# The second image's 3x3 convolution in transformed tiles of two rows by four columns

## The chip, the cores and the metric

One core of a Trainium2 chip runs the whole program. The metric is device microseconds from start to end of one execution; the time before is the median of three runs. Profiles come from one execution each, and their times are counted from the start of its span.

Engine names are those of the profile: PE is TensorE's products and PEld its weight loads, DVE is VectorE, ACT is ScalarE, POOL is GpSimd, SP is the queue that issues most transfers.

## What is computed

Two images of 256 channels and 64x64 pixels pass through two residual layers. Each layer normalises its input over groups of channels first.

```python
# layer 0: x += attention with 8 heads over all 4096 pixels
x = x + attention0(group_norm(x))
# layer 1, on h = group_norm(x):
q, k, v = c1x1(h, conv1), c1x1(h, conv2), c1x1(h, conv3)
ctx   = sa(blockify(q * hd**-0.5 + pos), blockify(k + pos), blockify(v))   # "first attention", groups of 64 pixels
feats = relu(c1x1(ctx, lr_W) * scale + shift)
qx, kx = two 1x1 layers each, with scale, shift and relu, of feats          # fq1, fq2 and fk1, fk2
vx    = c1x1(feats, sr_fv)
feats2 = relu(c1x1(sa(qx, kx, vx), sr_W) * scale + shift)                   # "second attention"
f_conv = per-head mixture of q, k, v by fc_w
out_conv = conv3x3(f_conv, dep_w, grouped)                                  # linear in h
x = x + rate1 * unblock(feats2) + rate2 * out_conv
```

Since q, k and v are linear in h, the mixture and the grouped 3x3 are one dense 3x3 convolution of h with 256 channels in and out; the kernel builds its weights itself.

## The kernel before

**Stages.** The images follow each other. For each: statistics and `project0` (the products `p_wk`, `p_wq`, `pv` of layer 0), `attention0` (its score products `ring`, its value products `av`, the exponent on ACT), then `layer1_first` (first attention, tiles named `lr`) and `layer1_second` (second attention, tiles named `sr`, together with the 3x3). In layer 1 the 4096 pixels are eight tiles `t` of 512 columns (eight image rows); `xts[t]` holds the residual `x` of tile `t`.

**A tile of the second attention.** `branch` makes `phq`, then `hq` on ACT, `prq`, then `rq`; the same for k. `group_attention` makes values (`pvs`), scores (`sp`), the softmax on DVE and ACT (`nm`, `e`, `den`, reciprocal, `e`), turns it on PE (`at`), copies it into a block-diagonal `bd` on DVE, and makes `pc`, which ACT turns into `res`.

**The 3x3.** Normalised pixels lie in `xp`, a zero-bordered image that `to_image` fills from the tiles. `conv_transform` and `conv_step` compute outputs in tiles of two rows by two columns from four row positions r and four column positions q. A step `(s, q)` handles a strip s of 16 rows and one q. `conv_transform` makes column combinations `col` (one POOL instruction, L1022) and row combinations `v` (four, L1026). `conv_step` makes 16 products of 256 columns into `mm`, four PSUM banks with a single buffer (L1036), drains them into `z` with one ACT copy and four DVE additions or subtractions (L1043 to L1047), and adds `z` to `xts` with strides of two (L1059, L1063, L1065). There are 16 steps per image.

```python
for r in range(4):
    for m in range(2):
        for k in range(KC):
            nc.tensor.matmul(mm[:, m, r, :], wf[:, k, 4 * r + q, m * P : (m + 1) * P],
                             v[r // 2][:, r % 2, k, :], start=k == 0, stop=k == KC - 1)
```

Weights `wf` (16 positions) are built on DVE in image 0 (`conv_weights`, L957), passed through memory (`wf_kept`), and fetched again for image 1.

**What sets the order.** Each engine works through its own queue in a fixed order. In `layer1_second` the order on PE is that of the program text (`manual_schedule`); a planner orders DVE, ACT, POOL and SP by its own cost estimates and by `issue_after`. `spots` says at which of three places of a tile a step `conv()` stands, and `images` in which tile further parts of `xp` are written. Step n issues the transform of step n+1. `give(n)` adds `rate1 * res + x` and writes the output of tile n once its strip is complete. Buffers come from rotating pools: `w4` (12 buffers of 4 KB per partition, for `v`, `z`, `hq`, `rq`, `res` and others), `xpool` (nine tiles), `cpool` (one, for `col`), `vpool` (one, for `wf`).

**The seams.** Between stages PE has little to hide behind. At the start, statistics (`pm`, `pv`, a square root on ACT) lead to the normalised `xn` and to `p_wk`; `fold_scores` makes the three small products `pt_place`, `pt_meet`, `pt_key` in between. `Stats.spread` makes a deviation `d` from `mean`. Between the two attentions of image 1, `feats` must be whole before `phq`.

Of the kernel before, what the change touches and what calls it, by code (L numbers as in the profile page):

```python
# [41 lines left out]
def direct_layers(ctx: ExitStack, tc: tile.TileContext, a: dict, out: bass.AP, bad: bass.AP):  # L42
# [19 lines left out]

    def open_banks(name, first):
        stack = ExitStack()
        places = range(first, 8)
        psum.update(
            turn=0, first=first,
            banks={i: stack.enter_context(tc.tile_pool(name=f"{name}_{i}", bufs=1, space=PSUM)) for i in places},
        )
        return stack  # L70
# [35 lines left out]
    def load_layer0(b):  # L106
        both = w4([P, 2, KC, NH0 * HD0], f"wqk0_{b}")
        w0 = {"wk0": both[:, 0], "wq0": both[:, 1]}
        for nm in w0:
# [4 lines left out]
            for k in range(KC):  # L114
                by_head = (by_row if b else rows)[:, k, :].rearrange("p (h m) -> p h m", m=2 * HD0)[:, :, 0:HD0]
                dst = w0[nm][:, k, :].rearrange("p (h m) -> p h m", m=HD0)
                if b:
                    nc.gpsimd.dma_start(out=dst, in_=by_head)
                else:
                    nc.scalar.copy(dst, by_head)  # L120
# [22 lines left out]
    nc.gpsimd.memset(eps, 1e-5)  # L143

# [178 lines left out]
    class Stats:  # L323
# [22 lines left out]
        def spread(self, ks):  # L346
            d = self.d[:, ks]
            nc.vector.tensor_sub(d, self.mv[:, ks, 0], self.mean[:, ks])
            nc.vector.tensor_mul(d, d, d)
            nc.vector.tensor_add(d, d, self.mv[:, ks, 1])  # L350
# [4 lines left out]
        def deviations(self, ks, pv):  # L355
            nc.scalar.activation(self.rstd[:, ks], pv, AF.Sqrt, bias=eps)
            nc.vector.reciprocal(self.rstd[:, ks], self.rstd[:, ks])

    def group_stats(xts, tagn):
# [8 lines left out]
        st.means(both, bank([P, KC], f"pm_{tagn}"), nc.vector.tensor_copy)  # L368
        st.spread(both)
# [3 lines left out]
        st.deviations(both, pv)  # L373
# [50 lines left out]
    def project0(b, xn, w0):  # L424

        def heads4(nm, g):
            for t in range(NT):
# [4 lines left out]
                for k in range(KC):  # L432
                    nc.tensor.matmul(  # L433
# [4 lines left out]
                nc.scalar.activation(pair[:, 0, :], pq, AF.Identity, bias=bias)  # L438
# [6 lines left out]
                )  # L445

        heads4("wk0", 0)
# [556 lines left out]
    kept = {}  # L1004
# [24 lines left out]
    def conv_step(b, xts, wf, v, s, q, pacc, behind_products=None):  # L1029
# [17 lines left out]
        nc.vector.tensor_sub(z[:, 1], z[:, 1], mm[:, :, 3, :])  # L1047
        bias = kept["bias"][1]
        for half in range(2):
            xs = xts[2 * s + half].rearrange("p m (i r j c) -> p m i r j c", i=4, r=2, c=2)  # L1050
            for r in range(2):
# [3 lines left out]
                for c in range(2):  # L1055
# [8 lines left out]
                    elif (q, c) in ((2, 1), (3, 1)):  # L1064
                        nc.vector.tensor_sub(dst, dst, zs)  # L1065

# [22 lines left out]
    def group_attention(nm, q, k, tokens, wv, out, busy=False, apart=False, more=None, split=False, fill=None, ends=None):  # L1089
# [36 lines left out]
        for t in range(4):  # L1126
            for c in range(KC):
                for par in range(2):
                    dst, n = place_of(t, par)
                    nc.tensor.matmul(  # L1130
                        dst, q[:, c, n], k[:, c, n], start=c == 0 and (t == 0 or not more),
                        stop=not more and c == KC - 1, skip_group_check=bool(more),
                    )
# [35 lines left out]
        for tt in range(2):  # L1169
            rows = slice(64 * tt, 64 * tt + 64)  # L1170
            nc.vector.tensor_copy(
# [48 lines left out]
    def layer1_first(b, put, check, st, groups):  # L1220
# [53 lines left out]
        with tc.manual_schedule(engines={E.PE, E.Activation, E.DVE, E.Pool}):  # L1274
# [7 lines left out]
            st.means(second, bank([P, 1], f"pm_l1_{b}"), nc.vector.tensor_copy)  # L1282
            st.spread(second)
# [17 lines left out]
        with tc.manual_schedule(engines={E.PE}):  # L1301

            before = None
            for t in range(NT + 1):
# [25 lines left out]
                before = parts  # L1330

# [4 lines left out]
    def layer1_second(b, xts, feats, mean, rstd, shift, pacc, following):  # L1336

        xp = apool.tile([P, KC, PADW, PADW], F32, tag="A", name=f"xp_{b}")
        for k in range(KC):
# [3 lines left out]
            nc.gpsimd.memset(xp[:, k, 1 : PADW - 1, 0 : PADW : PADW - 1], 0.0)  # L1343

        def to_image(t, both=False):
            for k in range(KC):
                dst = xp[:, k, 1 + 8 * t : 9 + 8 * t, 1 : 1 + W]
                src = xts[t][:, k, :].rearrange("p (r w) -> p r w", w=W)
                if both and k == 1:
# [7 lines left out]
        turns = [divmod(n, 4) for n in range(4 * NT // 2)]  # L1357
# [6 lines left out]
            t: (0, 1, 2) if t < 2 else (0, 1) for t in range(NT - 1)  # L1364
        }
        images = {1: range(5), 3: (5, 6), 4: (7,)} if b == 0 else {0: (3, 4), 1: (5,), 2: (6,), 3: (7,)}

        def conv(behind_products=None):
# [3 lines left out]
            if done + 1 < len(turns):  # L1372
                ahead[done + 1] = conv_transform(b, xp, *turns[done + 1])
            conv_step(b, xts, wf, ahead.pop(done), *turns[done], pacc, behind_products)
            done += 1

        def give(n):
# [3 lines left out]
            for m in range(KC):  # L1381
                nc.vector.scalar_tensor_tensor(
                    res[:, m, :], res[:, m, :], wts["rate1"], xts[n][:, m, :], ALU.mult, ALU.add
                )
# [5 lines left out]
        if b:  # L1390
            with tc.issue_after(kept["feats"].ins):
                for t in range(3):
                    to_image(t, True)
            ahead[0] = conv_transform(b, xp, *turns[0])
        pending, then = None, following()
        for t in range(NT):
# [5 lines left out]
            def branch(one, two, col1, col2, nm, between=None):  # L1402
                hid = w4([P, KC, T], f"h{nm}_{nt}")
                ph = [bank([P, T], f"ph{nm}_{nt}_{m}") for m in range(KC)]
                for k, m in ((0, 0), (0, 1), (1, 0), (1, 1)) if t == 0 else ((0, 0), (1, 0), (0, 1), (1, 1)):
# [3 lines left out]
                    if k == KC - 1:  # L1409
                        bn_relu(hid[:, m, :], ph[m], col1, m)  # L1410
# [21 lines left out]
            with tc.manual_schedule(engines={E.PE, E.DVE} if near else {E.PE}):  # L1432
                q = branch("fq1", "fq2", V_FQ1, V_FQ2, "q")
# [4 lines left out]
                for tt in images.get(t, ()):  # L1438
                    to_image(tt)
# [6 lines left out]
                if b == 0 and t == 2:  # L1446
                    conv()
                res = w4([P, KC, T], f"res_{nt}")
# [14 lines left out]
                next(parts)  # L1463
# [30 lines left out]
            for n in sorted(n for n in results if done >= 4 * (n // 2 + 1)):  # L1494
# [7 lines left out]
    def following():  # L1502
# [21 lines left out]
        st.means(both, bank([P, KC], "pm_l0_1"), nc.vector.tensor_copy)  # L1524
        st.spread(both)
# [10 lines left out]
    for b in range(B):  # L1536
        xts = x_first if b == 0 else ahead["xts"] + load_x(1, range(NT - 1, NT))
        w0 = w0_first if b == 0 else ahead["w0"]
        with open_banks(f"ps0_{b}", 0):
# [9 lines left out]
            next(fold, None)  # L1549
            held = project0(b, xn, w0)  # L1550
# [574 lines left out]
```

## Time and profile before

| what | value |
|---|---|
| median of three runs | 3026.41 us (3025.38 to 3028.41) |
| the profiled execution | 3024.22 us, span 3022.4 us |
| mean granted clock of PE | 0.998 |
| busy: PE, DVE, ACT, POOL | 98%, 81%, 77%, 28% of the span |
| image 0: attention of layer 0 | about 112 to 1120 us |
| image 0: layer 1 | about 1120 to 1528 us |
| image 1: attention of layer 0 | about 1640 to 2624 us |
| image 1: first attention, second attention with 3x3 | about 2624 to 2729 us, 2729 to 3015 us |
| product step L1036, image 1 | 512 records in 16 steps, mean duration 381 ns, overlapping |
| POOL: one `col`, one `v`, image 1 | 2146 ns, 1319 ns |
| DVE: one drain L1044 to L1047 | 678 to 688 ns |

Busy shares are averages over stages with different limits. Durations of single instructions overlap with their neighbours on the same engine, so the distance between starts is what a row of them costs. A product in fp32 stands in the trace as two records. The rows of one engine's waits name what came last before the wait ended.

### The profile page before, as it was taken

To read this page: it belongs to the slowest core of one execution; us is meant where nothing else is said; L and a number is where in the kernel's file an instruction comes from. 1 tells how busy PE (TensorE), PEld (TensorE's weight loads), DVE (VectorE), ACT (ScalarE), POOL (GpSimd) and SP (SyncE) were. 2 spreads that over 40 slices of the span, in tenths; PEclk is the share of its full clock that TensorE was granted. 3 is DMA by queue.
4 is the path that set the end of the run, shared out by engine and by line. 5 is a ranking of instruction groups with operands and counts; after the bars stand their busy time and mean duration, and the time that the engine had idled before them with its cause. 6 is when DMAs were issued, how large, how long until landed. Compare 5 with 4: busy or idle time off the path is not lost.

```text
span 3022.4 us, 64069 instructions
## 1 busy us (share of the span) xinstructions
PE 2963.0 (98%) x25161; PEld 1850.1 (61%) x25161; DVE 2443.4 (81%) x3111; ACT 2341.5 (77%) x3288; POOL 843.3 (28%) x930
## 2 busy tenths in 40 slices
PE   7999999999999999999999999999999999999998
PEld 4565556665565656577765555666555565576765
DVE  4698998999899999856647989989988899935543
ACT  2699999999999994622237999999999999844333
POOL 1022222322223230065401223222222222306440
PEclk9999999999999999999999999999999999999999
DMA  7979779897897761230169688797888976700000
GB/s 263 278 138 183 148 158 173 158 185 155 169 179 156 157 137 36 76 141 31 49 222 265 131 172 166 158 178 148 172 169 161 185 159 128 175 13 4 22 15 23
DMA packets 246662, 425.55 MB, mean 141 GB/s; under 512 B 99096, under 2 KB 110156, under 8 KB 244172
## 3 DMA queue, kind: packets, MB, share of 16 engines
q0 software_dynamic: 96960, 237.57, 40.8%
q1 hardware_dynamic: 149244, 183.51, 22.0%
q8 instruction: 199, 3.26, 0.5%
q14 instruction: 115, 0.94, 0.1%
q10 hardware_dynamic: 144, 0.26, 0.0%
HBM read 120.08 MB, written 68.39 MB: 62 GB/s over the span
## 4 chain that ended last, share of the span: by engine, by line
PE 87%; DVE 5%; DMA 3%; ACT 2%; issue 1%; SPq 0%; ACTq 0%; DVEq 0%; POOLq 0%
PE ring L567 32%; PE av L582 29%; PE mm L1036 7%; PE p_wk L433 2%; PE pv L456 2%; PE p_wq L433 2%; DVE prep L957 2%; PE prq_sr L1417 2%; PE prk_sr L1417 2%; PE pvs_sr L1106 2%; PE phk_sr L1406 1%; PE phq_sr L1406 1%; PE ring L582 1%; PE pvs_lr L1106 1%; PE py L1243 1%
## 5 line engine op out<-in xcount | busy, mean ns | idle before, releaser
L573 ACT ACTIVATE es<-ring 128x512 f32<-128x512 f32 (+2 forms) x1574 | 1202.3, 909 | 35.4 <-PE ring L567 23.3
L567 PE MATMUL ring<-q,k 128*128 128x512 f32 x4096 | 1083.9, 407 | 7.3 <-ACT es L573 5.4
L619 DVE TENSOR_TENSOR e<-e,es 128x1024 f32<-128x1024 f32 (+1 forms) x942 | 1028.8, 1153 | 28.4 <-ACT es L573 27.4
L567 PEld LDWEIGHTS ring<-q,k 128*128 128x128 f32 x4096 | 731.2, 188 | 382.7 <-ACT es L573 116.4
L573 ACT ACTIVATE v<-ring 128x512 f32<-128x512 f32 (+2 forms) x1036 | 785.6, 896 | 15.6 <-PE ring L567 7.5
L582 PE MATMUL av<-es,v 128*32 128x256 f32 (+1 forms) x9648 | 722.1, 389 | 0.0
L619 DVE TENSOR_TENSOR e<-e,v 128x1024 f32<-128x1024 f32 (+1 forms) x624 | 669.1, 1128 | 18.3 <-ACT v L573 17.6
L582 PE MATMUL av<-v 128*32 128x256 f32 x6224 | 506.0, 389 | 0.0
L582 PEld LDWEIGHTS av<-es,v 128*32 128x32 f32 x9648 | 325.2, 109 | 263.8 <-issue 105.1
L582 PEld LDWEIGHTS av<-v 128*32 128x32 f32 x6224 | 222.2, 109 | 169.8 <-issue 70.3
L1036 PE MATMUL mm<-v,wf 128*128 128x256 f32 x1024 | 227.6, 380 | 2.0 <-DVE z L1047 2.0
L629 POOL DMA_DIRECT2D es<-es x116 | 99.0, 853 | 438.5 <-ACT es L573 412.7
L1036 PEld LDWEIGHTS mm<-v,wf 128*128 128x128 f32 x1024 | 192.9, 190 | 33.7 <-issue 6.9
L1026 POOL TENSOR_TENSOR v<-col 128x512 f32<-128x512 f32 x128 | 165.3, 1317 | 172.8 <-ACT rk_sr L1195 40.3
L629 POOL DMA_DIRECT2D acc<-es x126 | 129.5, 1033 | 116.4 <-ACT es L573 32.1
L1043 ACT COPY z<-mm 128x512 f32<-128x512 f32 x32 | 18.7, 585 | 179.1 <-PE mm L1036 179.1
L627 POOL DMA_DIRECT2D es<-es x20 | 11.4, 568 | 508.6 <-ACT es L573 241.1
L629 POOL DMA_DIRECT2D es<-v x74 | 63.1, 853 | 291.1 <-ACT v L573 265.6
L1044 DVE TENSOR_TENSOR z<-z,mm 128x512 f32<-128x512 f32 x32 | 21.9, 686 | 125.3 <-ACT z L1043 124.9
L629 POOL DMA_DIRECT2D v<-es x114 | 115.3, 1011 | 24.7 <-ACT es L573 8.9
L629 POOL DMA_DIRECT2D acc<-v x86 | 87.5, 1017 | 81.9 <-DMA acc<-es 35.5
L1022 POOL TENSOR_TENSOR col<-xp 128x1152 f32<-128x1152 f32 x32 | 69.3, 2165 | 66.6 <-DVE xp L1487 55.4
(252 smaller groups left out, 2639.2 us busy)
## 6 DMA issues: line engine op xcount, KB each, us to landing
acc<-es POOLq DMA_DIRECT2D x122, 512.0 KB, 6.3
acc<-v POOLq DMA_DIRECT2D x78, 512.0 KB, 6.2
es<-es POOLq DMA_DIRECT2D x136, 256.0 KB, 4.2
v<-es POOLq DMA_DIRECT2D x134, 256.0 KB, 5.3
k<-wk_halves SPq DMA_DIRECT2D x64, 512.0 KB
q<-wq_halves SPq DMA_DIRECT2D x256, 128.0 KB
v<-v POOLq DMA_DIRECT2D x88, 256.0 KB, 4.8
es<-v POOLq DMA_DIRECT2D x86, 256.0 KB, 3.9
```

What stands on the lines that cost most here:

```text
L433: nc.tensor.matmul(pq, w0[nm][:, k, g * P : (g + 1) * P], xn[:, k, n], start=k == 0, stop=k == KC - 1)
L456: nc.tensor.matmul(pv[:, j, :], xn[:, k, n0 : n0 + P], w0["wv0"][:, k, :], start=k == 0, stop=k == KC - 1)
L567: touch(nc.tensor.matmul(sc[:, i, :], held["k", g // 2][:, j * P : (j + 1) * P], held["q", g, u // 2][:, u % 2, :], start=True, stop=True, ...
L573: nc.scalar.activation(dst, sc, AF.Exp, scale=SC0), set(range(at % BANKS, at % BANKS + m))
L582: note(nc.tensor.matmul(dst[HD0 * u : HD0 * u + HD0, n], lhs, rhs(u)[:, n], start=start, stop=stop))
L619: nc.vector.tensor_add(dst[:, s, :], dst[:, s, :], src)
L629: nc.gpsimd.dma_start(out=dst, in_=src, accum_op=ALU.add)
L1022: (nc.gpsimd.tensor_add if plus else nc.gpsimd.tensor_sub)(col, cols(one), cols(two))
L1026: (nc.gpsimd.tensor_add if plus else nc.gpsimd.tensor_sub)(dst, rows(one), rows(two))
L1036: nc.tensor.matmul(mm[:, m, r, :], wf[:, k, 4 * r + q, m * P : (m + 1) * P], v[r // 2][:, r % 2, k, :], start=k == 0, stop=k == KC - 1,)
L1106: nc.tensor.matmul(pv[:, i, :], tokens(c, 2 * half + i), wv[:, c, :], start=c == 0, stop=c == KC - 1)
L1417: nc.tensor.matmul(pr[m], wts[two][:, k, m * P : (m + 1) * P], hid[:, k, :], start=k == 0, stop=k == KC - 1)
```

## The change

For image 1 alone, the 3x3 works on tiles of two rows by four columns: six column positions q instead of four, on strips of 32 rows instead of 16. That is 2 strips x 6 = 12 steps, in the order q = 0 to 5 and then 5 to 0, each again with 16 products of 256 columns.

- **Column phases.** `x` and `xp` of image 1 are laid out by column modulo 4. `layer1_first` copies each tile of `x` into that layout on DVE while the first attention runs (`xphase`), `to_image` writes it (images 0 to 2 half on DVE and half on ACT, 3 and 4 on DVE, all ahead of the second attention; 5 to 7 in tiles 1 and 2), and `give` reads it back into column order. `rate1` is multiplied into `res` by an instruction of its own.
- **Transform.** `col` needs a POOL instruction of 1088 elements, two DVE instructions of 544 and one of 1088; `v` is four POOL instructions as before.
- **Step.** Products go to `mm[:, r, :, m, :]`, four pieces of 64 columns in a bank. Each `z` is added to up to four phases of four tiles: 16 instructions of 256 elements for q = 1 to 4, four for q = 0 and 5.
- **Weights.** Two more column positions are made from the four in image 0 (`wider_weights`, tiles 3 and 4, 16 DVE instructions and eight writes on SP). `WideWeights` keeps four positions and fetches the others when one is used up.
- **Order.** In both images, tile 0 makes `hq` and `hk` first; image writes in later tiles are issued after the first layer's rows. Additions of a step may be held until after the next drain (`held`); image 0's first step stands between scores and softmax. At the start three idle products run on arriving `x` and two more around the statistics, the `wk0` copies stand before the square root, the exponent's table is loaded by a one-column activation `warm`, and `pt_place`, `pt_meet`, `pt_key` move behind `p_wk`. `means_and_spread` makes `d` from PSUM directly. The last tile's scores loop over channels first. Image 1's tile 0 of `x` is loaded later, its buffer being used as `stage`.

```diff
+        idle = bank([P, T], "idle")
+        def keep_awake(t, n=T):
+            nc.tensor.matmul(idle[:, 0:n], ident, xts[t][:, 0, 0:n], start=True, stop=True)
+        for t in range(NT - 3, NT):
+            keep_awake(t)
+        st.means_and_spread(both, bank([P, KC], f"pm_{tagn}"))
...
+        with tc.issue_after(kept["compact"].ins):
+            root = st.deviations(both, pv)
+        with tc.issue_after(root.ins):
+            nc.scalar.activation(warm, eps, AF.Exp)
...
+    def wider_weights(wf, r, stage):
+        parts = [stage[:, n, :].rearrange("p (k c) -> p k c", k=KC) for n in range(2)]
+        one, two = parts
+        w = [wf[:, :, 4 * r + q, :] for q in range(4)]
+        nc.vector.scalar_tensor_tensor(one, w[3], 4.0, w[0], ALU.mult, ALU.add)
+        nc.vector.tensor_sub(two, w[1], w[2])
+        nc.vector.scalar_tensor_tensor(one, two, 2.0, one, ALU.mult, ALU.add)
+        nc.vector.scalar_tensor_tensor(two, two, -4.0, one, ALU.mult, ALU.add)
+        for n in range(2):
+            nc.sync.dma_start(out=wf_more[:, n, :, r, :], in_=parts[n])
...
+    class WideWeights:
+        TURNS = [(0, q) for q in range(NQ)] + [(1, q) for q in reversed(range(NQ))]
+        NEXT = {(0, 0): 4, (0, 1): 5, (1, 5): 1, (1, 4): 0}
...
+    def wide_transform(b, xp, s, q):
...
+        col = cpool.tile([P, KC, 34, WIDE], F32, tag="col", name=f"col_{b}_{s}_{q}")
...
+        (nc.gpsimd.tensor_add if plus else nc.gpsimd.tensor_sub)(col, cols(one), cols(two))
+        for k in range(KC):
+            nc.vector.scalar_tensor_tensor(
+                col[:, k], col[:, k], by, cols(third)[:, k], ALU.mult, ALU.add if third_plus else ALU.subtract
+            )
+        nc.vector.tensor_add(col, col, cols(fourth))
+        v = [w4([P, 2, KC, STRIP], f"v_{b}_{s}_{q}_{n}") for n in range(2)]
+        terms = ((0, 2, False), (1, 2, True), (2, 1, False), (1, 3, False))
+        for r, (one, two, plus) in enumerate(terms):
+            dst = v[r // 2][:, r % 2].rearrange("p k (i j) -> p k i j", j=WIDE)
+            (nc.gpsimd.tensor_add if plus else nc.gpsimd.tensor_sub)(dst, rows(one), rows(two))
...
+    def wide_step(b, xts, wide, v, s, q, pacc, behind_products=None):
+        mm = pacc.tile([P, 4, 4, 2, STRIP // 4], F32, tag="acc", name=f"mm_{b}_{s}_{q}")
...
+                    nc.tensor.matmul(
+                        mm[:, r, :, m, :], wide.of(q)[:, k, r, m * P : (m + 1) * P], v[r // 2][:, r % 2, k, :],
+                        start=k == 0, stop=k == KC - 1,
+                    )
+        wide.used(s, q)
...
+        nc.vector.tensor_add(z0, z1, products(0))
+        nc.vector.tensor_add(z0, z0, products(2))
+        nc.vector.tensor_sub(z1, z1, products(2))
+        nc.vector.tensor_sub(z1, z1, products(3))
+        yield
+        for t in range(4):
+            xs = xts[4 * s + t].rearrange("p k (a c j) -> p (k a) c j", c=NC, j=WIDE)
+            zs = z[:, t].rearrange("p m (a j) -> p (m a) j", j=WIDE)
+            for c, by in enumerate(BY[q]):
+                if by:
+                    nc.vector.scalar_tensor_tensor(xs[:, :, c, :], zs, by, xs[:, :, c, :], ALU.mult, ALU.add)
...
+                if b and t:
+                    new = xpool.tile([P, KC, T], F32, tag="x", name=f"xphase_{t - 1}")
...
+                        for k in range(KC):
+                            nc.vector.tensor_copy(phases(new)[:, k], old[:, k])
...
-            t: (0, 1, 2) if t < 2 else (0, 1) for t in range(NT - 1)
+            0: (1, 2), 1: (0, 1), 2: (0, 1), 3: (0, 1), 4: (0, 1), 5: (1,), 6: (1,)
         }
-        images = {1: range(5), 3: (5, 6), 4: (7,)} if b == 0 else {0: (3, 4), 1: (5,), 2: (6,), 3: (7,)}
+        images = {1: range(5), 3: (5, 6), 4: (7,)} if b == 0 else {1: (5, 6), 2: (7,)}
...
+            additions = step_of(b, xts, wf, ahead.pop(done), *turns[done], pacc, behind_products)
+            next(additions)
+            held.append(additions)
+            if behind_drain:
+                behind_drain()
+            else:
+                while held:
+                    next(held.pop(0), None)
...
+                for t in range(3):
+                    to_image(t, (1,))
+                for t in range(3, 5):
+                    to_image(t, (0, 1))
+            ahead[0] = transform(b, xp, *turns[0])
...
+                if t == 0:
+                    hids = {"q": hidden("fq1", V_FQ1, "q"), "k": hidden("fk1", V_FK1, "k")}
...
-                if b == 0 and t == 2:
-                    conv()
...
-                next(parts)
+                if b == 0 and t == 2:
+                    conv(behind_drain=lambda: next(parts))
+                else:
+                    next(parts)
```

## The prediction

> **What bounds the kernel now.** I read four views, in this order: the page's busy shares, the busy time by stretch of time, the chain of work that ended last, and TensorE's waits with the groups of the stage that changes.
>
> ```profile
> PE 2963.0 (98%) x25161; PEld 1850.1 (61%) x25161; DVE 2443.4 (81%) x3111; ACT 2341.5 (77%) x3288; POOL 843.3 (28%) x930
> PE 87%; DVE 5%; DMA 3%; ACT 2%; issue 1%; SPq 0%; ACTq 0%; DVEq 0%; POOLq 0%
> 2624.00:2729.00 105.00, 100.52 (x908) 70.74 (x908) 47.97 (x108) 50.06 (x69) 11.10 (x13) 1.00 0.14 51
> 2729.00:2759.00 30.00, 26.21 (x107) 15.09 (x107) 9.28 (x10) 15.54 (x22) 24.46 (x17) 0.94 0.00 1
> 2759.00:2910.00 151.00, 149.78 (x678) 107.50 (x679) 79.67 (x165) 48.14 (x87) 73.61 (x51) 1.00 0.04 15
> 2910.00:3015.00 105.00, 102.46 (x517) 71.43 (x515) 42.72 (x92) 37.53 (x67) 19.05 (x14) 1.00 0.05 17
> ```
>
> TensorE is busy nearly throughout, and the chain runs through it. In the stretch rows (us, then busy us of PE, PEld, DVE, ACT, POOL, then clock, DMA share, GB/s) the second image's second attention with the 3x3, 2729 to 3015, has TensorE full, VectorE about half full, and one hole at its start. So what TensorE no longer does there shortens the run, as long as VectorE, which receives new work, keeps up.
>
> ```profile
> 2861.10 6.91 PE mm L1036 x32
> 2877.68 7.10 PE mm L1036 x32
> 2736.68 5.40 PE prq_sr L1417 x8
> 2780.36 3.43 PE prq_sr L1417 x8
> PE prq_sr L1417 <- ACT hq_sr L1195: 2.8, 1, 2.8
> PE at_sr L1162 <- DVE e_sr L1157: 2.5, 1, 2.5
> 112.10 1.28 ACT L573 ACT_TABLE_LOAD   x1
> 2752.55 8.41 DVE L1059 SCALAR_TENSOR_TENSOR x<-z,edges,x 128x128 f32<-128x128 f32 x7
> 2775.37 0.60 DVE L1059 SCALAR_TENSOR_TENSOR x<-z,edges,x 128x128 f32<-128x128 f32 x2
> 2750.60 5.10 POOL L1026 TENSOR_TENSOR v<-col 128x512 f32<-128x512 f32 x4
> ```
>
> The chain gives a product step (16 matrix products, 32 records) 6.91 to 7.15 us, mean 7.0. The waits show two holes that the reordering touches. The last three rows are the danger: seven additions took 8.41 us while GpSimd worked, two took 0.60 us while it rested.
>
> **What the Trainium skill says.** "GPSIMD Engine Reference", section 1 (Specifications), says that GpSimd shares its SBUF interfaces with VectorE, and that VectorE instructions with two SBUF inputs contend; the rows above agree (about 1.2 us each against 0.3). "TensorE: Matmul & The Clock Gate", Part 1, says that an idle TensorE falls to half its clock and needs some 3.4 us of work to return; the trace agrees: after 2.8 us idle, prq took 5.40 us instead of 3.43. "ScalarE: Activation LUTs", What ACT_TABLE_LOAD costs, gives 1283 ns for a table load; the row above shows 1.28 us. "VectorE: DVE Perf Modes", the perf-mode tier table, says an fp32 tensor_tensor runs at one element a cycle; the trace's 256-element additions start 0.33 to 0.34 us apart and its 512-element ones from PSUM 0.61 to 0.72.
>
> **The change part by part**, against the profiled execution's 3024.2 us (its span is 3022.4).
>
> (1) Product steps. Image 1 makes 12 steps in place of 16, each again 16 products of 256 columns: 4 x 7.0 = **28.1 us less**, all on the chain. Not shown is a product written to PSUM as four pieces of 64. Between the same speed and a tenth slower (12 x 0.7 = 8.4 us lost; a gain is excluded, the columns being as many) I take the same.
>
> (2) The seam into the second attention, image 1. In the old trace the last pc_lr ended at 2729.1 and sp_sr of tile 0 at 2758.9, with one product step inside: 22.9 us without it. hq waited behind image writes on ScalarE, and the clock fell. In the new order of ScalarE's queue three such writes remain ahead of hq, and TensorE does phk meanwhile. Walk: feats to 2730.7, phq to 2733.0, phk to 2736.5, prq to 2739.9, prk to 2743.3, half the values to 2745.0, sp to 2746.1. That is 17.0: **5.9 less**.
>
> (3) The start. p_wk began at 23.88 behind place, meet, key and two wqk copies on ScalarE; now those copies stand ahead of the square root, and xn decides (about 22.0): 1.9. Its 32 records took 15.5 us, the next 32 13.9: idle products before it keep the clock, 1.5. The three small products move between p_wk and p_wq, 0.9 back. The exponent's table, 1.28 on the chain at 112, is loaded early. Together **3.8 less**; between 1 (wk_rows lands late, or the root's table now loads at the wrong moment) and 5.
>
> (4) Image 0. The softmax is put ahead of the first held additions (7.4 us of L1059 in the chain at 1311.7), so the 2.5 us wait of at_sr goes: **2.5 less**. Nothing from its seam, since the weights, built on VectorE until 1283 and landed at 1299, decide when products start. Making the extra weights is 16 VectorE instructions of 512 elements, some 11 us, beside 145 busy of 227 (1301 to 1528): nothing; if they are in the way, 5.
>
> (5) Hidden in image 1. Sixteen phase copies, about 0.55 us each by the L382 pace, lie in 105 us of which VectorE uses 48. The 16 multiplications by rate1 (0.35 to 0.55 each) replace nothing on the path before the last tile. SP gets 8 more writes, 8 loads in place of 4, and 8 refetches; DMA is at 0.00 to 0.14 there. A refetched pair is 1 MB, about 3 us by the pace of the x loads (4.2 MB in 12.5), issued at least two steps (some 28 us) before use. Statistics lose two short hops and split scores half a us, the last output gains an instruction of 0.4: **0.5 less**. The old waits between 2745 and 3015 (1.1 and 0.2) go too: **1.3 less**.
>
> (6) New on VectorE and GpSimd. A transform is now a GpSimd col (2146 ns x 1088/1152 = 2.0), two VectorE instructions of 544 elements and one of 1088 (0.64 + 0.64 + 1.2 = 2.5), and four v of 1.27 (5.1). Additions are 16 of 256 elements at 0.335 = 5.4 per inner step, drains 2.6 as before. A tile with two steps has 20.3 us of other products + 14.0 = 34.3 for TensorE, and for VectorE 2 x (2.5 + 2.6 + 5.4) + 3 softmax + 1 rate1 = 25, up to 32 if GpSimd blocks 3.5 a step. It fits in the steady state; I add 1.5 for marginal softmaxes.
>
> It does not fit in tile 0. VectorE's queue there reads: col_0_1, nm, e, den, col_0_2, reciprocal, col_0_2, e, add, bd, three drains of step 0, col_0_3, the fourth drain. GpSimd cannot be that far. Walk: images to 2733.0; col_0_0 to 2735.2, VectorE to 2737.7, v to 2742.9; col_0_1 to 2745.0, VectorE to 2747.5, v to 2752.7; col_0_2 to 2754.7. Only then come reciprocal and e, to 2756.6, while mm_0_0 ended at 2753.2: at_sr waits **3.5**. v_0_2 runs to 2763.0, col_0_3 to 2765.0, so the fourth drain ends at 2766.4; TensorE was through at 2761.4 and its four banks are not free: mm_0_1 waits **5.0**. Behind each wait I put 2 us of low clock, as at prq: **4**. From step 3 on GpSimd (9.6 us a transform) is ahead of steps about 17 us apart.
>
> Sum: -28.1 - 5.9 - 3.8 - 2.5 - 0.5 - 1.3 + 8.5 + 4 + 1.5 = **-28.1**: 2996.1 for such an execution. The profiled one lies 2.2 below the median 3026.4, so the median should be **2998**.
>
> **The rivals.** (A) The walk of tile 0 is too strict, its waits are hidden: 14 us less, 2984. For it: the old queue also mixed engines and lost only 1.3; against: the order is fixed at build. (B) The shared SBUF interface becomes the bound in tiles 0 to 4, which hold 10 of 12 steps: VectorE 10 x 2.5 + 26 + 124 x 0.335 + 15.5 + 10 = 118, GpSimd 10 x 7.15 = 71.5, and if nothing overlaps 189.5 against TensorE's 171.7: 18 back, 3016. For it: the 8.41 us row; against: v runs beside the drains, which read PSUM. (C) Slower: the coupling of tile 0 never loosens. Every step then costs a wait as in tile 0, 12 x (4.25 + 2) = 75 in place of 14: 3059. It decides from the point where a transform with its waits exceeds the 17 us between steps; 9.6 speaks against, buffers freed late speak for it. (D) The change doesn't do what it says: the pieces of 64 in PSUM slow a record by a third, 12 steps cost what 16 did, the 28.1 are gone: 3026.
>
> **How the numbers follow.** Forecast 0.50, A 0.20, B 0.20, C 0.06, D 0.04. A measurement of this kernel tells about 0.2% (6 us) from no change. Faster is forecast, A and B: 0.90; the same is D: 0.04; slower is C: 0.06. The range 2981 to 3014 takes in the forecast with the bounds of (1), (3) and (4), A, and the milder half of B.
>
> **What would show it.** Right: 192 products of the wide step in steps of 7.0 us; the hole at 2733 to 2737 gone; two new TensorE waits in tile 0, at_sr on e_sr and mm on the fourth drain, a few us each, and hardly any in later tiles; p_wk starting near 22 with all its records at one pace; no table load at the first exponent. Wrong: records of the step slower than 0.22 us apart, waits on drains or e_sr in tiles 1 to 4 that sum to over 15 us, or additions at over 1 us as a rule.

## The result, and the profile after

The changed kernel takes 3012.53 us (median of six runs, 3007.92 to 3016.01), the kernel before 3025.41 beside it; the ratio is 0.9955 (95% interval 0.9944 to 0.9965). It is faster, by 12.9 us where 28.1 were forecast. The profiled execution after took 3011.38 us; its span of 3009.5 is 12.9 us shorter than the one before, so the missing 15 us can be looked for in these two traces.

Both traces at the same events (us from the span's start, by the timeline):

| event | before | after | shift |
|---|---|---|---|
| first score product `ring` of image 0 | 111.46 | 112.84 | +1.4 |
| first product step `mm` of image 0 | 1301.1 | 1301.6 | +0.5 |
| first `p_wk` of image 1 | 1518.1 | 1530.7 | +12.6 |
| end of the last `ring` product of image 1 | 2630.3 | 2642.8 | +12.5 |
| end | 3022.4 | 3009.5 | -12.9 |

So image 1's layer 1 gave back 25.5 us (392.1 to 366.7; forecast 21.8), image 0's second attention lost 12.1 (217.0 to 229.0; forecast a gain of 2.5), and the start gained nothing (forecast 3.8; the first exponent, which no longer has a table load ahead of it, begins at 113.36 for 113.39). Differences of 1 to 3 us inside the long attentions come and go between executions of the same code, as the experiments show below.

The page after, busy shares and chain by engine:

```profile
PE 2945.0 (98%) x25043; PEld 1830.7 (61%) x25043; DVE 2499.7 (83%) x3196; ACT 2336.1 (78%) x3283; POOL 815.0 (27%) x910
PE 86%; DVE 6%; DMA 4%; ACT 2%; POOL 1%; issue 1%; SPq 0%; ACTq 0%; POOLq 0%; DVEq 0%
```

TensorE does 18 us less and VectorE 56 us more, but the chain spends a larger share on VectorE (6% for 5%) and on transfers (4% for 3%). The stretches of image 1, in the columns of the rows before (us, busy of PE, PEld, DVE, ACT, POOL, clock, DMA share, GB/s):

```profile
2636.00:2741.00 105.00, 100.46 (x914) 70.52 (x907) 56.40 (x123) 48.40 (x66) 11.19 (x13) 1.00 0.16 51
2741.00:2771.00 30.00, 25.81 (x114) 16.06 (x113) 12.51 (x21) 11.63 (x16) 17.09 (x12) 0.95 0.11 36
2771.00:2910.00 139.00, 136.00 (x606) 95.07 (x605) 106.28 (x195) 48.37 (x86) 65.19 (x45) 0.99 0.11 38
2910.00:3002.00 92.00, 90.01 (x458) 60.28 (x456) 47.91 (x109) 38.74 (x72) 5.00 (x4) 1.00 0.05 18
```

In the steady part (third row) TensorE is all but full, and VectorE is busy 106 of 139 us: it keeps up. The one hole is tile 0: the idle time of the second row (25.8 busy of 30) and 2.6 us at the start of the third. The chain of work that ended last, pieces from the start, from tiles 3 and 4 of image 0, and from image 1 (start, us, what):

```profile
21.28 1.28 ACT L368
...
23.76 15.65 PE p_wk L457 x32
...
1372.97 2.17 DMA wf_more<-stage
...
1381.03 8.83 PE mm L1062 x32
...
1421.52 2.98 DMA wf_more<-stage
...
1431.19 9.94 PE mm L1062 x32
...
2792.72 6.91 PE mm L1180 x32
...
2809.30 7.10 PE mm L1180 x32
```

The last two rows are what was bought: a step of the wide 3x3 takes the 6.91 to 7.1 us of an old one. The four before them are the new loss. In image 0 the chain leaves TensorE for VectorE's `stage` instructions and for the write of `stage` to memory, and the product steps behind them take 8.8 and 9.9 us in place of 6.9. TensorE's waits, image 0 (first row) and image 1 (us in total, times, longest):

```profile
PE mm L1062 <- DVE z L1073: 10.6, 3, 7.0
...
PE at_sr L1308 <- DVE e_sr L1303: 3.7, 1, 3.7
PE mm L1180 <- issue: 2.6, 1, 2.6
```

The two waits of image 1 are the forecast ones of tile 0; nothing like them follows in tiles 1 to 4. For the second the profile names no releaser (`issue`): its `v` had been ready since 2765.5, and the fourth drain of the step before ended at 2779.46, 0.1 us ahead of the first product, so I read it as the wait for that drain. The 10.6 us in image 0 stood at 0.9 before:

```profile
PE mm L1036 <- DVE z L1047: 0.9, 1, 0.9
```

GpSimd's and VectorE's timelines behind tile 4 of image 0 show why (start, us, instruction, idle time before it and what ended it):

```profile
1411.47 6.32 POOL L1052 TENSOR_TENSOR v<-col 128x512 f32<-128x512 f32 x4 [7.01 <-PE pc_sr L1328]
...
1424.33 2.92 POOL L1052 TENSOR_TENSOR v<-col 128x512 f32<-128x512 f32 x2 [3.99 <-ACT rq_sr L1341]
...
1411.12 2.17 DVE L1092 TENSOR_TENSOR x<-x,z 128x256 f32<-128x256 f32 x3
1413.22 1.75 DVE L1103 TENSOR_TENSOR stage<-wf 128x512 f32<-128x512 f32 x1
1414.90 1.75 DVE L1555 SCALAR_TENSOR_TENSOR res_sr<-res_sr,rate,x 128x512 f32<-128x512 f32 x1
1416.57 1.76 DVE L1104 SCALAR_TENSOR_TENSOR stage<-stage 128x512 f32<-128x512 f32 x1
1418.26 2.62 DVE L1555 SCALAR_TENSOR_TENSOR res_sr<-res_sr,rate,x 128x512 f32<-128x512 f32 x1
1420.81 0.68 DVE L1105 SCALAR_TENSOR_TENSOR stage<-stage 128x512 f32<-128x512 f32 x1
...
1424.52 1.61 DVE L1103 TENSOR_TENSOR stage<-wf 128x512 f32<-128x512 f32 x1 [1.11 <-DMA wf_more<-stage]
1426.17 1.62 DVE L1104 SCALAR_TENSOR_TENSOR stage<-stage 128x512 f32<-128x512 f32 x1
1427.72 0.68 DVE L1070 TENSOR_TENSOR z<-z,mm 128x512 f32<-128x512 f32 x1
```

The last row is the first drain of a step whose products had ended at 1419.0. Ahead of it in the queue stand seven of this tile's eight `stage` instructions and the additions of two results. Those that meet GpSimd's `v` take 1.6 to 1.76 us in place of 0.68, and one waits until the single buffer `stage` has been written to memory. `mm` has one set of banks, so TensorE can't begin the next step before the drains.

Two rows of PE's timeline answer the hole of the old seam, where `prq` took 5.40 us behind a wait:

```profile
2745.47 3.60 PE L1582 MATMUL phk_sr<-feats,wt_fk 128*128 128x512 f32 x8
2748.91 3.60 PE L1597 MATMUL prq_sr<-hq_sr,wt_fq 128*128 128x512 f32 x8
```

And VectorE's timeline in image 1 answers the slowed additions: sixteen of them with GpSimd at work for the first 0.4 us only, and sixteen beside the end of `v` and a `col`, 3.1 us together.

```profile
2790.44 5.75 DVE L1211 SCALAR_TENSOR_TENSOR xphase<-z,xphase 128x256 f32<-128x256 f32 x16
...
2803.10 8.13 DVE L1211 SCALAR_TENSOR_TENSOR xphase<-z,xphase 128x256 f32<-128x256 f32 x16
...
2798.93 5.00 POOL L1165 TENSOR_TENSOR v<-col 128x512 f32<-128x512 f32 x4 [8.05 <-DVE col L1160]
2804.01 2.25 POOL L1155 TENSOR_TENSOR col<-xp 128x1088 f32<-128x1088 f32 x1
```

### The profile page after: what moved, and what is told of

Its sections match the earlier page's. It is cut to its first block, busy times and chain, and to the rows that moved or that the text cites. A ratio compares the mean times of both kernels' runs of the same rounds, so it can differ in the third digit from the quotient of the medians.

```text
span 3009.5 us, 63901 instructions
## 1 busy us (share of the span) xinstructions
PE 2945.0 (98%) x25043; PEld 1830.7 (61%) x25043; DVE 2499.7 (83%) x3196; ACT 2336.1 (78%) x3283; POOL 815.0 (27%) x910
## 4 chain that ended last, share of the span: by engine, by line
PE 86%; DVE 6%; DMA 4%; ACT 2%; POOL 1%; issue 1%; SPq 0%; ACTq 0%; POOLq 0%; DVEq 0%
PE ring L594 32%; PE av L609 30%; PE mm L1062 3%; PE mm L1180 3%; PE p_wk L457 2%; PE p_wq L457 2%; DVE prep L984 2%; PE pv L483 2%; PE prq_sr L1597 1%; PE prk_sr L1597 1%; PE phk_sr L1582 1%; PE phq_sr L1582 1%; PE pvs_sr L1252 1%; DMA acc<-v 1%; PE ring L609 1%; PE pvs_lr L1252 1%
## 5 line engine op out<-in xcount | busy, mean ns | idle before, releaser
L1062 PE MATMUL mm<-v,wf 128*128 128x256 f32 x512 | 118.2, 391 | 10.6 <-DVE z L1073 10.6
L656 POOL DMA_DIRECT2D v<-es x114 | 116.2, 1019 | 25.6 <-ACT es L600 12.2
L1062 PEld LDWEIGHTS mm<-v,wf 128*128 128x128 f32 x512 | 99.5, 196 | 28.7 <-issue 14.5
L1052 POOL TENSOR_TENSOR v<-col 128x512 f32<-128x512 f32 x64 | 83.6, 1334 | 88.3 <-DVE x L1086 33.9
L1180 PE MATMUL mm<-v,wf 128*128 128x256 f32 x384 | 85.6, 381 | 2.6 <-issue 2.6
L984 DVE SCALAR_TENSOR_TENSOR prep<-prep 128x256 f32<-128x256 f32 x198 | 83.6, 477 | 0.4
L1165 POOL TENSOR_TENSOR v<-col 128x512 f32<-128x512 f32 x48 | 59.9, 1282 | 86.1 <-DVE col L1160 86.1
```

The lines of the kernel that those rows point to most:

```text
L656: nc.gpsimd.dma_start(out=dst, in_=src, accum_op=ALU.add)
L984: nc.vector.scalar_tensor_tensor(acc, src, s, acc, ALU.mult, ALU.add)
L1052: (nc.gpsimd.tensor_add if plus else nc.gpsimd.tensor_sub)(dst, rows(one), rows(two))
L1180: nc.tensor.matmul(mm[:, r, :, m, :], wide.of(q)[:, k, r, m * P : (m + 1) * P], v[r // 2][:, r % 2, k, :], start=k == 0, stop=k == KC - 1,)
```

## The experiments

Theory: the loss of image 0 comes from the `stage` instructions and their one buffer standing in VectorE's queue ahead of the drains; the start's gain did not come about because the root's table load moved onto the path; image 1 went as forecast. "First `mm` to `p_wk`" below is the stretch of image 0 from the table (before 217.0, after 229.0 us); "image 1" is the stretch from its last `ring` product to the end (before 392.1, after 366.7). Each ratio is to the kernel before, run beside it; that took 3025.3 to 3028.5 us, so medians of different experiments are better compared by their ratios or by these stretches. Without any change of their code, the stretch of image 0 took 228.9 to 229.2 us in six runs and that of image 1 366.1 to 368.4 in seven.

### The weights' instructions left out: n1_copies_only

```diff
-        parts = [stage[:, n, :].rearrange("p (k c) -> p k c", k=KC) for n in range(2)]
-        one, two = parts
-        w = [wf[:, :, 4 * r + q, :] for q in range(4)]
-        nc.vector.scalar_tensor_tensor(one, w[3], 4.0, w[0], ALU.mult, ALU.add)
-        nc.vector.tensor_sub(two, w[1], w[2])
-        nc.vector.scalar_tensor_tensor(one, two, 2.0, one, ALU.mult, ALU.add)
-        nc.vector.scalar_tensor_tensor(two, two, -4.0, one, ALU.mult, ALU.add)
         for n in range(2):
-            nc.sync.dma_start(out=wf_more[:, n, :, r, :], in_=parts[n])
+            nc.sync.dma_start(out=wf_more[:, n, :, r, :], in_=wf[:, :, 4 * r + n, :])
...
-                if t == 3:
-                    stage = xpool.tile([P, KC, T], F32, tag="x", name="stage")
+                stage = None
```

> The 16 VectorE instructions that make the extra weights in image 0 are left out (the 8 writes to memory stay, straight from the weights in place, so the second image's 3x3 uses wrong weights of the right size). Theory (VectorE's queue): these instructions and the wait for their one buffer stand ahead of the drains of tiles 3 and 4, where TensorE lost about 4.5 + 10 us; without them the wait of mm on z, 10.6 us in sum, falls under 2, the first p_wk of image 1 comes 12 to 14 us earlier (near 1528), and the median is 2998 to 3001. Rival (reordering): the loss comes from the additions held back behind the softmax and from GpSimd slowing VectorE there; then over 6 us of that wait stay and the median stays at 3008 to 3013.

Measured: 2999.94 us, ratio 0.9911 (0.9895 to 0.9928). First `mm` to `p_wk` took 214.5 us. The waits of image 0:

```profile
PE mm L1062 <- DVE z L1073: 0.9, 1, 0.9
```

All of the loss is gone, and the stretch is now 2.5 us shorter than before the change. That is the size of the wait of `at_sr` for the softmax, forecast to go, and no such wait is left. The reordering is no cause of the loss. The buffer goes together with the instructions here; the next runs part them. (`p_wk` itself came at 1520.8, since this execution reached its first `mm` 4.7 us later than the one after.)

### A second buffer: n3_two_stages

```diff
-                    stage = xpool.tile([P, KC, T], F32, tag="x", name="stage")
+                    stages = [xpool.tile([P, KC, T], F32, tag="x", name="stage")]
+                stages = [stages[0], w4([P, KC, T], f"stage_{t}")]
...
-                        wider_weights(wf, r, stage)
+                        wider_weights(wf, r, stages[r % 2])
```

> The two rows of one tile get a buffer each, so VectorE need not wait for the write to memory; the 16 instructions stay where they are. Theory (VectorE's queue, work and wait together): only the waits of 1.57 and 1.11 us go, and what follows from them on the clock, 3 to 5 us: 3008 to 3010, with 5 to 8 us of waits of mm on z left. Rival (the single buffer alone): nearly all waits of mm on z go: 2999 to 3001. Rival (reordering): no change, 3011 to 3013.

Measured: 3004.31 us, ratio 0.9924 (0.9907 to 0.9941); first `mm` to `p_wk` 219.8 us.

```profile
PE mm L1062 <- DVE z L1073: 4.3, 3, 2.6
```

Of the 14.5 us that the instructions cost, 9.2 go with the second buffer alone, and 5.3 stay. Neither theory had that split: I had put 3 to 5 on the buffer. VectorE's idle time at the buffer was only 2.7 us, but without it `stage` instructions also stand at other places of the queue: the last two of each tile now come behind the drains and additions of the second step.

### One row a tile: n2_one_a_tile

```diff
-            if b == 0 and t in (3, 4):
+            if b == 0 and t in (3, 4, 5, 6):
...
-                    for r in range(2 * (t - 3), 2 * (t - 3) + 2):
+                    for r in (t - 3,):
```

> The extra weights are made one row a tile in tiles 3 to 6 instead of two rows a tile in tiles 3 and 4. Theory (VectorE's queue): 4 instructions a tile fit into the slack between drains except in part in tile 4, where GpSimd slows them; the wait of mm on z falls from 10.6 to 1 to 4 us, and 8 to 13 us come back: 3000 to 3005. Rival (reordering): 3010 to 3013. Rival (the single buffer alone): the two waits for the write to memory, 2.7 us in sum, go with it, and with them all of the loss: 2999 to 3001.

Measured: 3009.86 us, ratio 0.9950 (0.9934 to 0.9967); first `mm` to `p_wk` 226.1 us. The theory and the single-buffer rival missed; the median lies next to the 3010 to 3013 of the reordering, which n1_copies_only has refuted. The reason is one that none had named. Behind the instructions of tile 3 TensorE no longer waits, behind those of tile 4 it waits 2.3 us, but a new wait of 6.2 us stands behind those of tile 6. Two rows of the timelines, VectorE and PE:

```profile
1509.04 1.29 DVE L341 BATCH_NORM_STATS2 stats_l<-x 128x6 f32<-128x512 f32 x2 [6.30 <-DMA x<-in_x_dram]
...
1513.30 9.47 PE L1062 MATMUL mm<-v,wf 128*128 128x256 f32 x32 [6.22 <-DVE z L1073]
```

A tile of the next image's `x` goes into the buffer that `stage` held, and its load waits for the last writes of `stage`. SP issued those from 1502.0 and the load at 1505.0; in the run after, the load that waits for `stage` left at 1433.3. The statistics wait for the load in VectorE's queue, and the drains wait behind the statistics. A late end of `stage` is paid for by a load.

### Spread over tiles 2, 3 and 5 with two buffers: f1_spread

```diff
-            if b == 0 and t in (3, 4):
-                if t == 3:
-                    stage = xpool.tile([P, KC, T], F32, tag="x", name="stage")
+            if b == 0 and t in (2, 3, 5):
+                if t == 2:
+                    spare = xpool.tile([P, KC, T], F32, tag="x", name="stage")
                 with tc.issue_after(kept["bd"].ins):
-                    for r in range(2 * (t - 3), 2 * (t - 3) + 2):
-                        wider_weights(wf, r, stage)
+                    for r in {2: (0,), 3: (1, 2), 5: (3,)}[t]:
+                        wider_weights(wf, r, w4([P, KC, T], f"stage_{r}") if r % 2 else spare)
```

> The extra weights keep all their instructions, but are made one row in tile 2, two in tile 3 and one in tile 5, none in tile 4, where GpSimd slows VectorE and two tiles of results are added, with two buffers in turn. Theory (VectorE's queue of tiles 3 and 4): the span from the first mm of image 0 to its last tile falls from 229 us to 215 to 218 as in the run without the instructions (214.5), the wait of mm on z from 10.6 to under 3, the median to 3000 to 3003. Rival (the amount of work: VectorE has no room for 16 instructions anywhere): 219 to 225 us there, and 3005 to 3010.

Measured: 3000.88 us, ratio 0.9918 (0.9899 to 0.9937); first `mm` to `p_wk` 215.6 us.

```profile
PE mm L1062 <- DVE z L1073: 1.8, 2, 0.9
```

All came as the theory expected. The same 16 instructions now cost 1.1 us in place of 14.5. VectorE has room for them; they stood at the wrong place, with a buffer too few.

### A product step made twice: d1_step_twice

```diff
-        for r in range(4):
+        for r in [*range(4)] * (2 if (s, q) in ((0, 3), (1, 3)) else 1):
```

> In image 1 the 16 products of two of the twelve steps, (0,3) and (1,3), are made twice into the same banks; nothing else is added. Theory (a product step is worth its 7.0 us on the path): image 1's second layer grows by 2 x 6.9 = 13.8 us, and the median to about 3026. Rival (VectorE or GpSimd sets the pace of tiles 1 to 4, and TensorE has slack there): under 8 us more, 3014 to 3020.

Measured: 3027.01 us, ratio 0.9996 (0.9987 to 1.0004); image 1 took 381.5 us, 14.8 more than after. That is 2 x 6.9 us for the two steps, and 1.2 by which the wait of `mm` in tile 0 was longer (3.8 for 2.6, as in f1_spread, whose image 1 has the same code as after). A step is worth its whole duration on the path, so the 28 us counted for four steps fewer stand.

### The old order at image 1's seam: t2_no_pair

```diff
-                if t == 0:
+                if t == 0 and b == 0:
                     hids = {"q": hidden("fq1", V_FQ1, "q"), "k": hidden("fk1", V_FK1, "k")}
```

> In image 1 the first hidden product of k is no longer put ahead beside that of q (phk stands behind prq again, as before the change; the rest of the seam stays). Theory (the order at the seam is worth what was forecast): TensorE waits for hq again, and the stretch from the last pc_lr to the first sp_sr, 16.1 us, grows by 2 to 5 us (2.8 us of wait and a slower prq behind it); the median rises by 2 to 5, to 3015 to 3017. Rival (ScalarE's shorter queue of image writes makes the order idle): under 1 us more, 3012 to 3013.

Measured: 3013.38 us, ratio 0.9960 (0.9947 to 0.9973). From the end of the last `pc_lr` row to the first `sp_sr` it takes 16.7 us for 16.1. The waits of image 1:

```profile
PE mm L1180 <- issue: 3.5, 1, 3.5
PE at_sr L1308 <- DVE e_sr L1303: 3.2, 1, 3.2
```

No wait for `hq` comes back, so the rival holds: putting `phk` ahead is worth 0.6 us there and nothing that the time can show. What is left as the cause is ScalarE's queue: before, six image writes of 4.31 us stood between `feats` and `hq`, now three of 2.21. No run put them back, so this is read from the two traces.

### The softmax of tile 0 first: t3_softmax_first

```diff
-                ahead[done + 1] = transform(b, xp, *turns[done + 1])
+                with tc.issue_after(kept["bd"].ins) if b and done == 1 else ExitStack():
+                    ahead[done + 1] = transform(b, xp, *turns[done + 1])
```

> In image 1, tile 0, the transform of the third turn (col_0_2) goes behind the softmax's last copy (bd) in VectorE's queue instead of between its steps. Theory: the wait of at_sr on e_sr (3.7 us) goes with the 1 to 2 us of low clock behind it; col_0_2 is needed only in tile 1 and comes 3 to 5 us later, which its own step can bear; the end comes 3 to 5 us earlier, 3008 to 3009. Rival (a wait that takes its place): the drains of step 0 now wait behind col_0_2, mm_0_1 waits 3 to 5 us more than its 2.6, and the time stays at 3012 to 3013.

Measured: 3009.62 us, ratio 0.9948 (0.9929 to 0.9967); image 1 took 365.3 us, 1.4 less, hardly below what the unchanged code takes. The waits of image 1:

```profile
PE at_sr L1308 <- DVE e_sr L1303: 3.8, 1, 3.8
PE mm L1180 <- POOL v L1165: 2.4, 1, 2.4
```

The wait of `at_sr` in tile 0 is gone, and the same one stands in tile 1: VectorE reaches the softmax there only at 2808.8, behind sixteen additions that come later and take 9.6 us beside GpSimd. In place of the wait for the drain one for the later `v` has come. A shift of one instruction group handed the wait to the next tile.

### Drains before every transform: t4_drains_first

On top of f1_spread:

```diff
-        nc.vector.tensor_sub(z1, z1, products(3))
+        kept["drained"] = nc.vector.tensor_sub(z1, z1, products(3))
...
-                ahead[done + 1] = transform(b, xp, *turns[done + 1])
+                with ExitStack() as behind:
+                    for last in ("bd", "drained") if b else ():
+                        if last in kept:
+                            behind.enter_context(tc.issue_after(kept[last].ins))
+                    ahead[done + 1] = transform(b, xp, *turns[done + 1])
```

> On top of f1_spread (3000.9): in image 1 every transform stands behind the last softmax copy (bd) and behind the last drain of the step before it in VectorE's queue. Theory (the order of tile 0's queue cost the waits): the waits of at_sr on e_sr in tiles 0 and 1 (3.7 and, in t3_softmax_first, 3.8) and of mm on a drain (2.6) go, with 2 to 3 us of low clock; the time from the end of the last ring of image 1 to the end falls from 367 us to 359 to 362, and the median to 2993 to 2997. Rival (the chain of GpSimd and VectorE through three transforms, some 10.3 us each, is what tile 0 waits for): one wait of mm on v takes their place, and the median stays at 2999 to 3001.

Measured: 2993.18 us, ratio 0.9891 (0.9875 to 0.9908); image 1 took 358.7 us, 8.0 less than after and 9.5 less than f1_spread (368.2), on which it stands.

```profile
PE at_sr L1308 <- DVE e_sr L1303: 1.2, 1, 1.2
```

The one wait that is left stands in tile 1. So the order in VectorE's queue set the waits of tile 0 and not the chain of transforms: with drains and softmax ahead, the transforms still arrive in time.

### The start: s1_root_first, s3_idle_twice and c1_both

```diff
     warm = const.tile([P, 1], F32, name="warm")
+    nc.scalar.activation(warm, eps, AF.Sqrt)
```

> A square root of one column is put first in ScalarE's queue, so that its table is loaded before any data is there. Theory: the load of 1.28 us that stands between pv and the square root goes, xn and the first p_wk come 1.3 us earlier (22.5 instead of 23.8), and the median falls by about 1.3 us, to 3011. Rival: something else decides the first p_wk (the copies of its weights, which now stand ahead on ScalarE): it stays at 23.5 to 23.9 and the time is unchanged.

Measured: 3012.53 us, ratio 0.9953 (0.9937 to 0.9970), the median of the changed kernel. The chain of s1_root_first at the start, and then what ScalarE waits for at the head of the first attention (100 to 172 us); in the changed kernel no wait for `acc` (transfers that add to what lies at their target) stands there.

```profile
20.33 0.27 ACT rstd_l L369
...
21.52 13.97 PE p_wk L458 x32
```

```profile
ACT v L601 <- DMA acc<-v: 2.3, 2, 1.3
...
ACT es L601 <- DMA acc<-es: 1.2, 2, 1.0
```

The table load was indeed on the path: without it `p_wk` starts at 21.5. The first `ring` comes at 108.93, 3.9 us earlier than in the changed kernel, and the first exponent at 109.44, 3.95 earlier than in the kernel before, about the 3.8 that I had forecast. Part of that is luck: the 32 records of `p_wk` took 13.97 us for 15.65 at a granted clock of 1.00 for 0.89, but f1_spread and t3_softmax_first had 13.97 and 1.00 as well, without this edit. And the first sum of `ring` with `ones`, at the end of the first unit, comes at 189.40 for 189.93 (190.01 in the kernel before). On the way ScalarE waits 3.5 us for accumulating copies that have not landed.

The opposite, with a later start:

```diff
-        for t in range(NT - 3, NT):
+        for t in [*range(NT - 3, NT)] * 2:
             keep_awake(t)
```

> The first three idle products at the start are issued twice, so that the first p_wk comes 2 to 5 us later than 23.8. Theory (what follows the start is paced by transfers): the first unit of the first attention ends at 190 to 191.5 whatever the start, as it did with first scores at 108.9 to 113.6, so the median stays within 2 us of 3012.5. Rival (the start lies on the path): the end moves by the whole delay, to 3015 to 3017.

Measured: 3016.62 us, ratio 0.9971 (0.9963 to 0.9979). `p_wk` came 1.95 us later, the first unit's end 5.9 us later. My theory that the end of that unit stays where it is has fallen for a later start. The rival, that it moves by the delay, doesn't explain 5.9 either. Here too ScalarE waits for the accumulating copies (4.2 us), so these waits are not the price of a head start alone.

c1_both is t4_drains_first with the edit of s1_root_first.

> t4_drains_first with the square root's table loaded first, as in s1_root_first. Theory (the first unit of the first attention is paced by its transfers, so an earlier start is given back there): p_wk starts at 21.5 in place of 23.5, but the median is within 1.5 us of t4_drains_first. Rival (the start is on the path, and s1_root_first only fell in slow transfers): 2 to 4 us less than t4_drains_first.

Measured: 2990.96 us, ratio 0.9881 (0.9865 to 0.9898), against 2993.18 without that edit: 2.2 less, by four runs each that overlap (2990.11 to 2993.09; 2992.71 to 2994.73), so the medians just reach the rival's 2 to 4 and miss the theory's 1.5. In the profiled executions the head start of 3.2 us at the first `ring` (109.26 for 112.46) is gone at the end of the first unit (190.95 for 190.92), and the spans are 2991.0 and 2990.6. What an earlier start is worth stays open between nothing and some 2 us, and so does what holds the first unit back. c1_both is the fastest version that I ran.

The first unit's length shows how loose that coupling is. From first `ring` to its end it takes 77.1 us after, 77.9 in f1_spread, 80.5 in s1_root_first and 81.1 in s3_idle_twice. The code of that unit is the same in all four.

## Why the prediction was right or wrong

The direction held and the mechanism of image 1 too. The size failed by 15.2 us, in two steps of the sum: image 0 (14.6 us worse than forecast) and the start (its 3.8 did not come). By chance too high a sum for image 1 made up 3.7 of it.

**(1) Product steps, 28.1: right.** The `mm` records of image 1 have a mean of 381 ns as before (384 of them), the pieces of 64 cost nothing, and d1_step_twice shows that a step counts in full. Rival D is refuted.

**(2) The seam, 5.9: nearly right.** My stretch of 17.0 us, from the last `pc_lr` to the end of `sp_sr`, took 18.1 (2740.61 to 2758.67), so 4.8 were gained; 1.0 of the missing 1.1 lies in `feats` and `phq`, which ended 4.9 us after that `pc_lr` and not 3.9. That `phk` now stands ahead was not the cause (t2_no_pair); the shorter queue of image writes is what remains.

**(3) The start, 3.8: failed.** I had named as a bound that the root's table could load at the wrong moment, and then priced it at no more than 2.8. It did. In the kernel before, the load stood ahead of the wait for `pv` and was over long before; the change put it behind that wait, 1.28 us on the chain:

```profile
2.78 1.28 ACT L356 ACT_TABLE_LOAD   x1
...
21.28 1.28 ACT L368 ACT_TABLE_LOAD   x1 [1.29 <-PE pv_l L365]
```

The idle products held `pv` until 21.1, so `p_wk` began at 23.76, not 22.0. Nor did they keep the clock: it was 0.89 over the records of `p_wk`, and in other runs of the same code 0.82 to 1.00. s1_root_first and c1_both add the second error: of the 3 to 4 us at the first score product, 0.5 was left at the end of the first unit in one run and nothing in the other. I had costed the start as if it were on the path throughout; why it isn't stays open.

**(4) Image 0: the gain right, the cover wrong.** This is the step that failed. The 2.5 us came (n1_copies_only). But "beside 145 busy of 227: nothing; if they are in the way, 5" was read from an average. That VectorE idles for 82 of those 227 us says nothing of what stands ahead of a drain: the 16 instructions were placed ahead of drains, half of them in a stretch where GpSimd slows VectorE, with one buffer that a write to memory must empty. They cost 14.5 us. I had the slowed row (8.41 us for seven additions) in front of me, and applied it to image 1 alone. The price has three parts that my bound left out: instructions at 1.6 to 1.76 us for 0.68, the buffer's wait, and TensorE's low clock behind a wait. The first two show in 9.7 us more of waiting, the third in steps of 8.83 and 9.94 us for 6.91, at a granted clock of 0.81 and 0.72: 14.6 in all. That last part agrees with "TensorE: Matmul & The Clock Gate", Part 1, as after the old seam: an idle TensorE falls to half its clock. But the page names an idle window of about 3.4 us, and here a wait of 2.6 us was enough.

**(5) Hidden work: right.** Phase copies, `rate1` and the fetches show up in no wait of TensorE. The small gains of 1.8 us that stand beside them in the sum were not measured.

**(6) Tile 0: the place right, the sum too high.** I gave 14 us: 3.5 for `at_sr` on `e_sr` (measured 3.7), 5.0 for `mm` on the fourth drain (2.6), 4 of low clock and 1.5 for marginal softmaxes. Between the two waits the products took 7.4 us, at a granted clock of 0.64, where the same row takes 4.6 in the next tile: 2.8. Behind the second wait the clock was full. That makes 9.1. Taking the order away agrees: t4_drains_first gave back 9.5 against the run on which it stands. With (1), (2) and the unmeasured 1.8 the sum closes: -28.1 - 4.8 - 1.8 + 9.1 = -25.6, where image 1 changed by -25.5.

**Rival B** landed close to the measured time, for a wrong reason: tiles 1 to 4 have no wait on VectorE to speak of. Its mechanism was at work, though, in image 0. Sixteen additions took 5.75 us almost alone and 8.13 with GpSimd beside them for 3.1, which again agrees with what "GPSIMD Engine Reference", section 1, says of shared interfaces. **Rival A** is refuted by tile 0's waits, **rival C** by the quiet tiles behind it.

## What to carry to other kernels

Work for an engine with free time is not free: ask at which place of its queue it will stand, what is queued behind it, and whether that is what the bounding engine waits for. Here the same 16 instructions cost 14.5 us ahead of the drains with one buffer, and 1.1 us spread out with two. And a head start into a long stage should be counted only if something at the end of that stage moves with it.

## What the runs showed of the hardware that I had not expected

- The same table load can lie inside a wait or behind it. In the kernel before it ran at 2.78 us, 18 us ahead of the root that needs it. In the changed kernel, where the root has an instruction of its own that waits (`ACTq L368`, 21.23), it began at 21.28, when `pv` was there (21.21), though ScalarE had had nothing to do since 20.0; with the same function called once at the start it was gone from the chain.
- TensorE's clock at the start isn't the same in every execution: from the first record of `p_wk` to the first of `p_wq` it took 15.8 us in the run after, 17.1 in n1_copies_only and 14.1 in f1_spread and t3_softmax_first, with the same instructions ahead of them.
- The long attention of image 0 varies by about 3 us between executions: from its first unit's end to its last sums it took 934.6 us in t3_softmax_first and 937.3 in n3_two_stages, with the same code. Effects of that size are read from a stretch of the trace and not from two spans.
